# A Macaron layer with a selective scan: giving its two FFNs row buffers of their own, and carrying rows and scan output through DRAM

## The chip, the cores and the metric

The kernel runs on one core of a Trainium2 chip. The metric is device microseconds of one execution; the median of several runs is given. One further execution was recorded by the hardware profiler; the profile below is of that one.

## What is computed

The input x has 2 sequences of 2048 positions and 1024 features, all in float32. Three residual steps follow each other:

```
x = x + 0.5 * ffn(layernorm(x))
x = x + mamba(layernorm(x))
x = x + 0.5 * ffn(layernorm(x))
```

Both FFNs have the same weights. For each position, `ffn` forms 64 vectors of 16 numbers (one 1024x1024 product with A), takes the 4 vectors with the largest norm, sums those 4 into one vector v, spreads it over the chosen ones, and returns `x W^T + bias + (spread v) B`: three 1024x1024 products in all. `mamba` projects to a step delta (rank 128, then softplus) and to B and C of 16 states, and runs

```
h[t] = exp(delta[t] * A) * h[t-1] + delta[t] * B[t] * x[t]
y[t] = sum over the 16 states of h[t] * C[t];   result: y + x * D_param
```

over the positions, for 1024 features x 16 states, starting at zero in each sequence.

## The kernel before, in words

The 4096 positions are cut into 16 chunks of 256, each of two row blocks of 128 positions. A row block lies in an SBUF tile x of 128 positions x 1024 features. For every chunk the program adds tasks in this order: `ffn("f", c, i)` for both row blocks (the first FFN), `prepare(c)`, `scans(c)`, and `ffn("g", c, i)` for both (the second FFN).

- `ffn` (from L486). An f block is loaded in two layouts by `load_rows` (L337): as rows (x) and transposed (xnt). A g block takes the x tile that the scan has added to, and turns it with 8 PE transposes (`turn`, L464). Statistics are made by DVE and ACT (L424 to L446). PE computes the products with A (wa), W (ww) and B (wb), all at L515, 16 of 128x512 each; each product leaves two records in the profile. In between ACT squares (L537), DVE selects (L551 to L574) and POOL spreads (L583). DVE adds the result into the x tile (`close`, L601), and a g block is stored (L613).
- `prepare` (from L619) normalizes the chunk's x, turns it into u, projects it, makes delta, and stores delta, u*delta, u, B and C in DRAM tiles (du_d, u_d, bc_d).
- `scans` (from L760) goes through 1024 features in four steps of two 128-feature blocks (q). In each it fetches du_d back, replicated fourfold over the partitions, into four rep tiles, and runs 16 tasks (4 groups of states hi x 4 groups of features j). A task is: ACT's exponential (`decay`, L808), DVE's product (`entry`, L816), DVE's recurrence (`scan`, L823, two instructions), ACT's copy of the last state (L833), POOL's product with C (`leave`, L836). After every four tasks PE sums states into y (L856). At the end of a step DVE adds u * D_param to y (`skip`, L869), PE turns the result (`back`, L877), and DVE adds it into the two x tiles of the chunk (`summed`, L886).

So an x tile is held from the load of an f block until the store of the same g block. There are six such tiles, and the f blocks of a chunk can be at most three chunks ahead of the g blocks.

The order on each engine is fixed before the kernel is built. Each task names an engine, a planned cost in us, what it reads and writes, a rank, and the places of pools it takes and gives back. `Plan.order` (L124) plays the program through with these costs: whenever an engine is free it takes the ready task of lowest rank whose places are free. DVE and POOL tasks marked `port` are not started while the other engine has such a task running. A transfer's places and results count as there when its planned landing time has passed. The tasks are then emitted in the order found, and on the chip each engine works through its own list strictly in that order, waiting where something isn't there yet. All transfers are issued by SP's queue.

Pools that matter: x 6; xnt 2; rep 5; h 10 (a task's state tile, given back by PE's sum at L856); ysb 2; the PSUM pools ff 3 and pt 2; the DRAM pools du_d, u_d and bc_d, 2 each. The rank of an f block comes from a list (`f_seq`, L329) in which the f blocks of chunk c + 3 stand beside the g blocks of chunk c.

Of the kernel before, what the change touches and what calls it, by code (L numbers as in the profile page):

```python
# [28 lines left out]
FP = mybir.dt.float32  # L29
# [6 lines left out]
P = 128  # L36
TC = 256
# [187 lines left out]
def macaron_kernel(  # L225
# [39 lines left out]

    places("x", 6, [P, D])
    places("row", 1, [P, D])
# [59 lines left out]

    xs, xts, ready = {}, {}, {}
    f_seq = [("f", c, i) for c in range(min(3, NCH)) for i in range(NT)]  # L329
# [7 lines left out]
    def load_rows(c, i):  # L337
        xs[c, i] = x_p = Place("x")
# [12 lines left out]

# [67 lines left out]
    def spread_of(x_p, st, factor, rank, after=()):  # L419
# [27 lines left out]

        add("DVE", 1.9, stats, row(x_p) + list(after), [(st, 0)], rank=-40.0 + rank, take=[st])
        add("ACT", 1.8, root, [(st, 0)], [(st, 1)], rank=-10.0 + rank)

    def normalize(x_p, xn_p, rank, after=()):

        st = Place("stats")
        spread_of(x_p, st, 1.0, rank, after)

        def scale():
            r, s = st.tile[:, 15:16], st.tile[:, 16:17]
            nc.scalar.activation(s, st.tile[:, 13:14], AF.Identity, scale=r)
            nc.scalar.activation(xn_p.tile, x_p.tile, AF.Identity, bias=s, scale=r)

        add("ACT", 1.45, scale, row(x_p) + [(st, 1)], [(xn_p, 0), (xn_p, 1)], rank=-10.0 + rank,
            take=[xn_p], give=[st])

    def turn(src, keys, dst, out_keys, rank, take=(), give_src=None):  # L464

        for g in range(2):
            pt = Place("pt")

            def pe(g=g, pt=pt):
                for k in range(HC):  # L470
                    c0 = (g * HC + k) * P
                    nc.tensor.transpose(  # L472
                        pt.tile[:, k * P : (k + 1) * P], src.tile[:, c0 : c0 + P], ident
                    )
# [4 lines left out]
            add("PE", 0.65, pe, keys(g) + ([(take[0], "-")] if take and g else []), [(pt, 0)],  # L479
                rank=-50.0 + rank, take=[pt] + (list(take) if g == 0 else []),  # L480
                give=[src] if give_src else [])
            add("ACT", 0.58, act, [(pt, 0)], out_keys(g), rank=-60.0 + rank, give=[pt])

    def ffn(kind, c, i):  # L486
        n = place_in[kind, c, i]
        rank = 0.01 * n
        if kind == "f":
            load_rows(c, i)  # L490
        x_p = xs[c, i]
        g_p, gt, ch, mk, st = (Place(k) for k in ("g", "gt", "choice", "marked", "stats"))
# [10 lines left out]
        for h in range(2):  # L503
            def bias(h=h):
                cols = slice(h * HD, (h + 1) * HD)
                nc.gpsimd.tensor_add(x_p.tile[:, cols], x_p.tile[:, cols], half_bias[:, cols])  # L506

            add("POOL", 1.3, bias, row(x_p, h) + ["half_bias"], row(x_p, h), rank=rank, port=True)
        turn_of = Turn()

        def products(ps, h, lhs, w, wn, start, stop, order, take, give, after=()):
            for k4 in range(KC // 4):
                def pe(k4=k4):
# [8 lines left out]

                add("PE", 3.6, pe,
                    [(lhs, k4)] + [(wn, k, h) for k in range(4 * k4, 4 * k4 + 4)]
# [21 lines left out]
        def choose():  # L546
# [12 lines left out]

        add("DVE", 2.2, choose, [(g_p, 0), (g_p, 1)], [(ch, 0)], rank=-50.0 + rank,  # L560
            take=[ch, mk], give=[mk])
        for h in range(2):
            def routed(h=h):
# [5 lines left out]

            add("DVE", 0.68, routed, [(pv[h], 0), (ch, 0)], [(g_p, h)], rank=-50.0 + rank,  # L570
                give=[pv[h]])
# [6 lines left out]

        add("DVE", 1.25, total, [(g_p, 0), (g_p, 1)], [(ch, 1)], rank=-50.0 + rank)
        for h in range(2):  # L580
            def spread(h=h):
# [6 lines left out]

            add("POOL", 1.3, spread, [(ch, 0), (ch, 1)], [(g_p, h)], rank=-30.0 + rank, port=True,
                give=[ch])  # L590
# [5 lines left out]
        for h in range(2):  # L596
            products(po, h, gt, wb, "wb", False, True, lambda: turn_of.number - 1000.0, [], [gt])

            def close(h=h):
# [5 lines left out]

            add("DVE", 0.68, close, [(po[h], 0), (st, 1)] + row(x_p, h), row(x_p, h),
                rank=-50.0 + rank, give=[po[h], st])
        if kind == "g":
            b, t = chunks[c]
# [9 lines left out]
    def prepare(c):  # L619
# [48 lines left out]
        def keep(p, pt, m):  # L668
            return lambda: nc.scalar.copy(p.tile[:m, :], pt.tile[:m, :TC])

        add("PE", 3.8, project, ["wx"] + u_all, [(pd, 0)], rank=-45.0 + rank, take=[pd])
        add("ACT", 0.38, keep(dr, pd, P), [(pd, 0)], [(dr, 0)], rank=-55.0 + rank, take=[dr],
            give=[pd])
        add("PE", 1.3, project_bc, ["wx"] + u_all, [(pb, 0)], rank=-45.0 + rank, take=[pb])
        add("ACT", 0.38, keep(bc, pb, P), [(pb, 0)], [(bc, 0)], rank=-55.0 + rank, take=[bc],
# [11 lines left out]
        for g in range(2):  # L687
            dg, e = Place("delta"), Place("row")
            for k2 in range(HC // 2):
# [10 lines left out]
                def parts(g=g, k2=k2, pt=pt, e=e, dg=dg):  # L700
# [5 lines left out]

                add("PE", 0.8, pz, [(dr, 0), "wdt"] + ([(e, "-")] if k2 else []), [(pt, 0)],
                    rank=-45.0 + rank, take=[pt] if k2 else [pt, e, dg], give=[dr])
                add("ACT", 1.85, parts, [(pt, 0), "bdt"], [(e, k2), (dg, k2)], rank=-55.0 + rank,
                    give=[pt])  # L710
# [29 lines left out]
            ukeys = [(u, g, i) for i in range(NT)]  # L740
            add("ACT", 1.1, exp, ek, ek, rank=-20.0 + rank)
# [3 lines left out]
            add("ACT", 3.7, log, ek, ek, rank=-20.0 + rank)  # L745
            add("DVE", 1.25, delta, ek + dk, dk, rank=-20.0 + rank, port=True, give=[e])
# [13 lines left out]
    def scans(c):  # L760

        du_d, bc_d, u_d = ready.pop(c)
        bs, cs = [Place("b") for _ in range(HI)], [Place("c") for _ in range(HI)]
        for hi in range(HI):
# [9 lines left out]
        for q in range(0, KC, 2):  # L774
            reps = [Place("rep") for _ in range(NJ)]
            for j in range(NJ):
                def fetch(q=q, j=j, r=reps[j]):
# [11 lines left out]
                    give=[du_d], land=4.0)  # L789
            y, ysb, pt = Place("y"), Place("ysb"), Place("pt")  # L790

# [8 lines left out]
            for hi in range(HI):  # L800
                hs = []
                for j in range(NJ):
# [32 lines left out]
                    def leave(h=h, hi=hi):  # L835
# [6 lines left out]
                    end = q == KC - 2  # L842
                    add("ACT", 1.0, decay, [(r, 0), "a_neg"], [(da, 0)], rank=-80.0 + rank, take=[da],
                        give=[r])
# [3 lines left out]
                    add("DVE", 1.36, scan, [(da, 0), (h, 0), key], [(h, 0)], rank=rank, give=[da])  # L848
                    add("ACT", 0.2, keep, [(h, 0)], [key, (h, 1)], rank=-90.0 + rank)
# [13 lines left out]

                add("PE", 1.0, total, [(h, 0) for h in hs], [(y, 0)], rank=-70.0 + rank,
                    take=[y] if hi == 0 else [], give=hs)
# [100 lines left out]
```

## Time and profile before

| | us |
|---|---|
| median of 3 runs | 3503.4 |
| lowest, highest | 3498.0, 3507.41 |
| the profiled execution, its own time | 3495.17 |
| its span in the profile | 3493.4 |
| mean granted TensorE clock | 0.986 |

The page of the profile lists, for each engine, its busy time in the span (PE is TensorE's matmuls, PEld its weight loads, DVE VectorE, ACT ScalarE, POOL GpSimd, SP SyncE), then 40 slices of the span with the busy share of each engine in tenths (9 is 90% or more), and the granted clock of TensorE in tenths. "Chain" is the work that ended last, followed back from the end. A group's line has its line in the kernel, engine and operation, the tiles it writes and reads, its shape and count; then busy time and the mean duration of one in ns; then the idle time of the engine ahead of it and what ended most of that. A queue's name with a q (SPq) means its sequencer.

Transfers take a 24% share of the 16 DMA engines over the span and move 285.70 MB. Median times from issue to landing: rep<-du_d 3.3 us, x<-in_x 4.5, ysb<-u_d 2.8, out<-x 2.6.

### The profile page before, as it was taken

To read this page: it belongs to the slowest core of one execution; us is meant where nothing else is said; L and a number is where in the kernel's file an instruction comes from. 1 tells how busy PE (TensorE), PEld (TensorE's weight loads), DVE (VectorE), ACT (ScalarE), POOL (GpSimd) and SP (SyncE) were. 2 spreads that over 40 slices of the span, in tenths; PEclk is the share of its full clock that TensorE was granted. 3 is DMA by queue.
4 is the path that set the end of the run, shared out by engine and by line. 5 is a ranking of instruction groups with operands and counts; after the bars stand their busy time and mean duration, and the time that the engine had idled before them with its cause. 6 is when DMAs were issued, how large, how long until landed. Compare 5 with 4: busy or idle time off the path is not lost.

```text
span 3493.4 us, 36224 instructions
## 1 busy us (share of the span) xinstructions
PE 3309.1 (95%) x10280; PEld 1456.1 (42%) x10280; DVE 3136.3 (90%) x4753; ACT 1882.0 (54%) x4818; POOL 1882.0 (54%) x1299
## 2 busy tenths in 40 slices
PE   7999798999998999999999999999999999999989
PEld 3444333444443444443443444444444444444434
DVE  5399999999999999998899999898989989899991
ACT  1365655556465555655564655565565555555541
POOL 1154566555465665645555566464555655465571
PEclk9999899999999999999999999999999999999999
DMA  5222222222223213222131221312222232222210
GB/s 201 90 71 81 96 82 67 94 85 67 80 77 99 73 62 112 70 85 82 58 103 61 97 82 58 124 58 97 67 97 70 69 110 69 95 70 74 72 58 12
DMA packets 182058, 285.70 MB, mean 82 GB/s; under 512 B 17120, under 2 KB 100704, under 8 KB 181856
## 3 DMA queue, kind: packets, MB, share of 16 engines
q1 hardware_dynamic: 181856, 283.38, 24.2%
q8 instruction: 81, 1.33, 0.2%
q14 instruction: 121, 0.99, 0.1%
HBM read 215.69 MB, written 67.63 MB: 81 GB/s over the span
## 4 chain that ended last, share of the span: by engine, by line
PE 44%; DVE 33%; issue 11%; ACT 9%; DMA 2%; SPq 0%; POOL 0%; DVEq 0%; POOLq 0%; ACTq 0%
PE ff L515 37%; DVE h L823 14%; DVE h L816 7%; PE y L856 3%; DVE stats L424 2%; ACT da L808 2%; ACT stats L445 1%; DVE norms L551 1%; DVE g L564 1%; PE pt L472 1%; ACT stats L446 1%; PE pt L695 1%; DMA rep<-du_d 1%; DVE x L601 1%; DVE x L886 1%
## 5 line engine op out<-in xcount | busy, mean ns | idle before, releaser
L836 POOL TENSOR_TENSOR h<-h,c 128x512 f32<-128x512 f32 x1024 | 1544.1, 1518 | 1057.2 <-ACT state L833 1002.2
L808 ACT ACTIVATE da<-rep,a_neg 128x256 f32<-128x256 f32 x2048 | 974.6, 477 | 956.0 <-DVE h L823 916.3
L823 DVE TENSOR_TENSOR_SCAN h<-da,state,h 128x256 f32<-128x256 f32 x2048 | 1384.4, 727 | 23.1 <-ACT da L808 19.3
L816 DVE TENSOR_TENSOR h<-rep,b 128x512 f32<-128x512 f32 x1024 | 968.6, 973 | 61.0 <-PE y L856 59.0
L515 PE MATMUL ff<-ww,xnt 128*128 128x512 f32 x2048 | 908.4, 600 | 28.6 <-DVE g L564 28.1
L515 PE MATMUL ff<-wa,xnt 128*128 128x512 f32 x2048 | 918.4, 597 | 0.4 <-ACT xnt L477 0.2
L515 PE MATMUL ff<-wb,gt 128*128 128x512 f32 x2048 | 899.0, 597 | 16.1 <-ACT gt L477 16.0
L515 PEld LDWEIGHTS ff<-ww,xnt 128*128 128x128 f32 x2048 | 390.7, 192 | 535.9 <-issue 476.7
L515 PEld LDWEIGHTS ff<-wb,gt 128*128 128x128 f32 x2048 | 386.8, 191 | 489.0 <-issue 460.1
L515 PEld LDWEIGHTS ff<-wa,xnt 128*128 128x128 f32 x2048 | 378.0, 190 | 480.6 <-issue 475.3
L583 POOL TENSOR_TENSOR g<-choice 128x512 f32<-128x512 f32 x128 | 162.9, 1292 | 323.9 <-DVE choice L574 323.9
L856 PE MATMUL y<-h,summer 128*32 128x512 f32 x2048 | 305.0, 609 | 30.1 <-POOL h L836 26.9
L506 POOL TENSOR_TENSOR x<-x,half_bias 128x512 f32<-128x512 f32 x128 | 173.6, 1368 | 186.9 <-DVE stats L424 164.0
L833 ACT COPY state<-h 128x2 f32<-128x2 f32 x1024 | 186.3, 182 | 110.1 <-DVE h L823 109.7
L537 ACT ACTIVATE g<-ff 128x512 f32<-128x512 f32 x128 | 133.7, 1046 | 115.7 <-PE ff L515 115.1
L601 DVE SCALAR_TENSOR_TENSOR x<-ff,stats,x 128x512 f32<-128x512 f32 x128 | 93.6, 732 | 81.8 <-PE ff L515 81.0
L424 DVE BATCH_NORM_STATS2 stats<-x 128x6 f32<-128x512 f32 x192 | 122.3, 677 | 40.5 <-DMA x<-in_x 40.4
L856 PEld LDWEIGHTS y<-h,summer 128*32 128x32 f32 x2048 | 51.6, 109 | 220.3 <-POOL h L836 111.0
L477 ACT COPY gt<-pt 128x512 f32<-128x512 f32 x128 | 69.8, 584 | 101.6 <-PE pt L472 101.6
L444 ACT ACTIVATE stats<-stats 128x1 f32<-128x1 f32 x288 | 58.2, 202 | 121.7 <-DVE stats L436 115.6
L445 ACT ACTIVATE stats<-stats,less 128x1 f32<-128x1 f32 x288 | 111.3, 386 | 9.7
L551 DVE TENSOR_REDUCE norms<-g 128x64 f32<-128x1024 f32 x64 | 76.8, 1199 | 27.0 <-ACT g L537 21.8
(73 smaller groups left out, 1753.2 us busy)
## 6 DMA issues: line engine op xcount, KB each, us to landing
rep<-du_d SPq DMA_DIRECT2D x512, 256.0 KB, 3.3
xnt<-in_x_t SPq DMA_DIRECT2D x32, 512.0 KB, 3.6
x<-in_x SPq DMA_DIRECT2D x32, 512.0 KB, 4.5
u_d<-u SPq DMA_DIRECT2D x32, 512.0 KB, 4.7
ysb<-u_d SPq DMA_DIRECT2D x64, 256.0 KB, 2.8
du_d<-delta SPq DMA_DIRECT2D x32, 512.0 KB, 3.2
du_d<-u SPq DMA_DIRECT2D x32, 512.0 KB, 3.0
out<-x SPq DMA_DIRECT2D x32, 512.0 KB, 2.6
```

The costliest lines, as they stand in the source:

```text
L424: nc.vector.bn_stats(st.tile[:, 6 * s : 6 * s + 6], x_p.tile[:, s * HD : (s + 1) * HD])
L445: nc.scalar.activation(t, q, AF.Identity, bias=less, scale=hv)
L506: nc.gpsimd.tensor_add(x_p.tile[:, cols], x_p.tile[:, cols], half_bias[:, cols])
L515: nc.tensor.matmul(ps[h].tile, lhsT=lhs.tile[:, k, :], rhs=w[:, k, h * HD : (h + 1) * HD], start=start and k == 0, stop=stop and k == KC - 1,)
L537: nc.scalar.activation(g_p.tile.rearrange("p (a r) -> p r a", r=RANK)[:, h * r2 : (h + 1) * r2, :], vecs(pv, h), AF.Square,)
L583: nc.gpsimd.tensor_mul(g_p.tile[:, h * HD : (h + 1) * HD].rearrange("p (r a) -> p r a", a=na), ch.tile[:, :NA].unsqueeze(1).to_broadcast([ ...
L808: nc.scalar.activation(da.tile[:, k, :], r.tile[:, k, 0, :], AF.Exp, scale=a_neg[:, q + k, j, hi : hi + 1],)
L816: nc.vector.tensor_mul(h.tile, r.tile[:, :, 1, :], bs[hi].tile.unsqueeze(1).to_broadcast([P, 2, TC]),)
L823: nc.vector.tensor_tensor_scan(h.tile[:, k, :], da.tile[:, k, :], h.tile[:, k, :], state[:, q + k, j, hi : hi + 1], ALU.mult, ALU.add,)
L833: nc.scalar.copy(state[:, q : q + 2, j, hi : hi + 1], h.tile[:, :, TC - 1 : TC])
L836: nc.gpsimd.tensor_mul(h.tile, h.tile, cs[hi].tile.unsqueeze(1).to_broadcast([P, 2, TC]))
L856: nc.tensor.matmul(y.tile[j * DB : (j + 1) * DB, :], lhsT=summer, rhs=hs[j].tile.rearrange("p k t -> p (k t)"), start=(hi == 0), stop=(hi ...
```

## The change

The six x tiles become three xf (first FFN), two xg (second FFN) and one yt (a row block's y, features on partitions). After `close`, an f block is stored in a DRAM tile x1_d, and its xf tile is given back when this store has landed and `prepare` has normalized it. The scan no longer turns y nor adds it: each step stores its y in a DRAM tile y_d. A new function `load_sum` fetches a g block's x and y, turns y in two groups of four transposes, and adds it to x. The DRAM pools du_d, u_d and bc_d have four tiles instead of two. Some 30 planned costs are altered; those move the order alone.

```diff
-    places("x", 6, [P, D])
+    places("xf", 3, [P, D])
+    places("xg", 2, [P, D])
+    places("yt", 1, [P, KC, P])
...
-    plan.pool("du_d", [dram.tile([D, 2, TC], FP, name=f"du_d{j}") for j in range(2)])
-    plan.pool("u_d", [dram.tile([D, TC], FP, name=f"u_d{j}") for j in range(2)])
-    plan.pool("bc_d", [dram.tile([2 * N, TC], FP, name=f"bc_d{j}") for j in range(2)])
+    plan.pool("du_d", [dram.tile([D, 2, TC], FP, name=f"du_d{j}") for j in range(4)])
+    plan.pool("u_d", [dram.tile([D, TC], FP, name=f"u_d{j}") for j in range(4)])
+    plan.pool("bc_d", [dram.tile([2 * N, TC], FP, name=f"bc_d{j}") for j in range(4)])
+
+    plan.pool("x1_d", [dram.tile([P, D], FP, name=f"x1_d{j}") for j in range(2 * NT * 4)])
+    plan.pool("y_d", [dram.tile([D, TC], FP, name=f"y_d{j}") for j in range(4)])
...
+    def load_sum(c, i, rank):
+
+        xs[c, i] = x_p = Place("xg")
+        yt = Place("yt")
+        x1_d, y_d = x1_ds.pop((c, i)), y_ds[c]
+
+        def fetch_x():
+            nc.sync.dma_start(out=x_p.tile, in_=x1_d.tile)
+
+        def fetch_y():
+            nc.sync.dma_start(
+                out=yt.tile,
+                in_=y_d.tile[:, i * P : (i + 1) * P].rearrange("(k p) t -> p k t", p=P),
+            )
+
+        add("SP", 0.4, fetch_x, [(x1_d, 0)] + [(y_d, q) for q in range(0, KC, 2)], row(x_p),
+            rank=-30.0 + rank, take=[x_p], give=[x1_d], land=3.0)
+        add("SP", 0.6, fetch_y, [(y_d, q) for q in range(0, KC, 2)], [(yt, 0)], rank=-30.0 + rank,
+            take=[yt], give=[y_d], land=4.0)
+        for g in range(2):
+            pt = Place("pt")
+
+            def back(g=g, pt=pt):
+                for k in range(HC):
+                    nc.tensor.transpose(
+                        pt.tile[:, k * P : (k + 1) * P], yt.tile[:, g * HC + k, :], ident
+                    )
+
+            def summed(g=g, pt=pt):
+                cols = x_p.tile[:, g * HD : (g + 1) * HD]
+                nc.vector.tensor_add(cols, pt.tile, cols)
+
+            add("PE", 0.56, back, [(yt, 0)] + row(x_p, g), [(pt, 0)], rank=-50.0 + rank, take=[pt], give=[yt])
+            add("DVE", 0.72, summed, [(pt, 0)] + row(x_p, g), row(x_p, g), rank=-45.0 + rank,
+                give=[pt])
...
-        add("ACT", 1.8, root, [(st, 0)], [(st, 1)], rank=-10.0 + rank)
+        add("ACT", 2.65, root, [(st, 0)], [(st, 1)], rank=-10.0 + rank)
...
-            take=[xn_p], give=[st])
+            take=[xn_p], give=[st, x_p])
...
+        else:
+            load_sum(c, i, rank)
...
-                add("PE", 3.6, pe,
+                add("PE", 3.44, pe,
...
-        if kind == "g":
+        if kind == "f":
+            x1_ds[c, i] = x1_d = Place("x1_d")
+
+            def keep():
+                nc.sync.dma_start(out=x1_d.tile, in_=x_p.tile)
+
+            add("SP", 0.4, keep, row(x_p), [(x1_d, 0)], rank=-50.0, take=[x1_d], give=[x_p],
+                land=3.0)
+        else:
...
-                    add("DVE", 0.68, entry, [(r, 0), (bs[hi], 0)], [(h, 0)], rank=rank - 0.0012,
+                    add("DVE", 0.66, entry, [(r, 0), (bs[hi], 0)], [(h, 0)], rank=rank - 0.0012,
...
-                    add("POOL", 1.3, leave, [(h, 1), (cs[hi], 0)], [(h, 0)], rank=-20.0 + rank,
+                    add("POOL", 1.26, leave, [(h, 1), (cs[hi], 0)], [(h, 0)], rank=-20.0 + rank,
...
-            def back(ysb=ysb, pt=pt):
-                for i in range(NT):
-                    for k in range(2):
-                        nc.tensor.transpose(
-                            pt.tile[:, (2 * i + k) * P : (2 * i + k + 1) * P],
-                            ysb.tile[:, k, i * P : (i + 1) * P],
-                            ident,
-                        )
-
-            def summed(q=q, pt=pt):
-                for i in range(NT):
-                    cols = xs[c, i].tile[:, q * P : (q + 2) * P]
-                    nc.vector.tensor_add(cols, pt.tile[:, 2 * i * P : 2 * (i + 1) * P], cols)
-
-            add("DVE", 0.8, skip, [(y, 0), (ysb, 0), "d_col"], [(ysb, 0)], rank=-45.0, give=[y])
-            add("PE", 0.65, back, [(ysb, 0)], [(pt, 0)], rank=-75.0 + rank, take=[pt], give=[ysb])
-            add("DVE", 0.84, summed, [(pt, 0)],
-                [(xs[c, i], k) for i in range(NT) for k in (q, q + 1)], rank=-45.0, give=[pt])
+            def put_y(q=q, ysb=ysb):
+                nc.sync.dma_start(
+                    out=y_d.tile[q * P : (q + 2) * P, :].rearrange("(k p) t -> p k t", p=P),
+                    in_=ysb.tile,
+                )
+
+            add("DVE", 0.86, skip, [(y, 0), (ysb, 0), "d_col"], [(ysb, 0)], rank=-45.0, give=[y])
+            add("SP", 0.4, put_y, [(ysb, 0)], [(y_d, q)], rank=-50.0, take=[] if q else [y_d],
+                give=[ysb], land=3.0)
```

More of the change, by code (lines that the diff above doesn't have):

```diff
@@ L326, in macaron_kernel @@
     plan.pool("marked", marked)
-    xs, xts, ready = {}, {}, {}
+    xs, xts, ready, x1_ds, y_ds = {}, {}, {}, {}, {}
     f_seq = [("f", c, i) for c in range(min(3, NCH)) for i in range(NT)]
@@ L337, in load_rows @@
     def load_rows(c, i):
-        xs[c, i] = x_p = Place("x")
+        xs[c, i] = x_p = Place("xf")
         xts[c, i] = xt = Place("xnt")
@@ L446, in root @@
                 nc.scalar.activation(r, t, AF.Identity, scale=r)
-        add("DVE", 1.9, stats, row(x_p) + list(after), [(st, 0)], rank=-40.0 + rank, take=[st])
-        add("ACT", 1.8, root, [(st, 0)], [(st, 1)], rank=-10.0 + rank)
+        add("DVE", 1.94, stats, row(x_p) + list(after), [(st, 0)], rank=-40.0 + rank, take=[st])
+        add("ACT", 2.65, root, [(st, 0)], [(st, 1)], rank=-10.0 + rank)
     def normalize(x_p, xn_p, rank, after=()):
@@ L459, in scale @@
             nc.scalar.activation(xn_p.tile, x_p.tile, AF.Identity, bias=s, scale=r)
-        add("ACT", 1.45, scale, row(x_p) + [(st, 1)], [(xn_p, 0), (xn_p, 1)], rank=-10.0 + rank,
-            take=[xn_p], give=[st])
+        add("ACT", 1.55, scale, row(x_p) + [(st, 1)], [(xn_p, 0), (xn_p, 1)], rank=-10.0 + rank,
+            take=[xn_p], give=[st, x_p])
     def turn(src, keys, dst, out_keys, rank, take=(), give_src=None):
@@ L477, in act @@
                 nc.scalar.copy(dst(g), pt.tile.rearrange("p (k t) -> p k t", k=HC))
-            add("PE", 0.65, pe, keys(g) + ([(take[0], "-")] if take and g else []), [(pt, 0)],
+            add("PE", 0.56, pe, keys(g) + ([(take[0], "-")] if take and g else []), [(pt, 0)],
                 rank=-50.0 + rank, take=[pt] + (list(take) if g == 0 else []),
                 give=[src] if give_src else [])
-            add("ACT", 0.58, act, [(pt, 0)], out_keys(g), rank=-60.0 + rank, give=[pt])
+            add("ACT", 0.585, act, [(pt, 0)], out_keys(g), rank=-60.0 + rank, give=[pt])
     def ffn(kind, c, i):
@@ L506, in bias @@
                 nc.gpsimd.tensor_add(x_p.tile[:, cols], x_p.tile[:, cols], half_bias[:, cols])
-            add("POOL", 1.3, bias, row(x_p, h) + ["half_bias"], row(x_p, h), rank=rank, port=True)
+            add("POOL", 1.26, bias, row(x_p, h) + ["half_bias"], row(x_p, h), rank=rank, port=True)
         turn_of = Turn()
@@ L558, in choose @@
             nc.vector.tensor_scalar(routes, routes, CHOSEN, 1.0 / TOPK, ALU.is_equal, ALU.mult)
-        add("DVE", 2.2, choose, [(g_p, 0), (g_p, 1)], [(ch, 0)], rank=-50.0 + rank,
+        add("DVE", 2.24, choose, [(g_p, 0), (g_p, 1)], [(ch, 0)], rank=-50.0 + rank,
             take=[ch, mk], give=[mk])
@@ L568, in routed @@
                 )
-            add("DVE", 0.68, routed, [(pv[h], 0), (ch, 0)], [(g_p, h)], rank=-50.0 + rank,
+            add("DVE", 0.65, routed, [(pv[h], 0), (ch, 0)], [(g_p, h)], rank=-50.0 + rank,
                 give=[pv[h]])
@@ L577, in total @@
             )
-        add("DVE", 1.25, total, [(g_p, 0), (g_p, 1)], [(ch, 1)], rank=-50.0 + rank)
+        add("DVE", 1.22, total, [(g_p, 0), (g_p, 1)], [(ch, 1)], rank=-50.0 + rank)
         for h in range(2):
@@ L587, in spread @@
                 )
-            add("POOL", 1.3, spread, [(ch, 0), (ch, 1)], [(g_p, h)], rank=-30.0 + rank, port=True,
+            add("POOL", 1.26, spread, [(ch, 0), (ch, 1)], [(g_p, h)], rank=-30.0 + rank, port=True,
                 give=[ch])
@@ L604, in close @@
                 )
-            add("DVE", 0.68, close, [(po[h], 0), (st, 1)] + row(x_p, h), row(x_p, h),
+            add("DVE", 0.73, close, [(po[h], 0), (st, 1)] + row(x_p, h), row(x_p, h),
                 rank=-50.0 + rank, give=[po[h], st])
-        if kind == "g":
+        if kind == "f":
[5 more added lines that the diff above has]
+        else:
             b, t = chunks[c]
@@ L669, in keep @@
             return lambda: nc.scalar.copy(p.tile[:m, :], pt.tile[:m, :TC])
-        add("PE", 3.8, project, ["wx"] + u_all, [(pd, 0)], rank=-45.0 + rank, take=[pd])
+        add("PE", 3.6, project, ["wx"] + u_all, [(pd, 0)], rank=-45.0 + rank, take=[pd])
         add("ACT", 0.38, keep(dr, pd, P), [(pd, 0)], [(dr, 0)], rank=-55.0 + rank, take=[dr],
             give=[pd])
-        add("PE", 1.3, project_bc, ["wx"] + u_all, [(pb, 0)], rank=-45.0 + rank, take=[pb])
+        add("PE", 1.05, project_bc, ["wx"] + u_all, [(pb, 0)], rank=-45.0 + rank, take=[pb])
         add("ACT", 0.38, keep(bc, pb, P), [(pb, 0)], [(bc, 0)], rank=-55.0 + rank, take=[bc],
@@ L705, in parts @@
                         nc.scalar.activation(dg.tile[:, k, :], z, AF.Relu, bias=bias)
-                add("PE", 0.8, pz, [(dr, 0), "wdt"] + ([(e, "-")] if k2 else []), [(pt, 0)],
+                add("PE", 0.93, pz, [(dr, 0), "wdt"] + ([(e, "-")] if k2 else []), [(pt, 0)],
                     rank=-45.0 + rank, take=[pt] if k2 else [pt, e, dg], give=[dr])
-                add("ACT", 1.85, parts, [(pt, 0), "bdt"], [(e, k2), (dg, k2)], rank=-55.0 + rank,
+                add("ACT", 1.92, parts, [(pt, 0), "bdt"], [(e, k2), (dg, k2)], rank=-55.0 + rank,
                     give=[pt])
@@ L740, in prepare @@
             ukeys = [(u, g, i) for i in range(NT)]
-            add("ACT", 1.1, exp, ek, ek, rank=-20.0 + rank)
+            add("ACT", 1.06, exp, ek, ek, rank=-20.0 + rank)
             add("DVE", 1.25, plus, ek + dk, dk, rank=-20.0 + rank, port=True)
@@ L744, in prepare @@
             add("DVE", 1.25, rest, ek + dk, dk, rank=-20.0 + rank, port=True)
-            add("ACT", 3.7, log, ek, ek, rank=-20.0 + rank)
+            add("ACT", 3.6, log, ek, ek, rank=-20.0 + rank)
             add("DVE", 1.25, delta, ek + dk, dk, rank=-20.0 + rank, port=True, give=[e])
@@ L762, in scans @@
         du_d, bc_d, u_d = ready.pop(c)
+        y_ds[c] = y_d = Place("y_d")
         bs, cs = [Place("b") for _ in range(HI)], [Place("c") for _ in range(HI)]
@@ L789, in scans @@
                     give=[du_d], land=4.0)
-            y, ysb, pt = Place("y"), Place("ysb"), Place("pt")
+            y, ysb = Place("y"), Place("ysb")
             def fetch_u(q=q, ysb=ysb):
@@ L842, in scans @@
                     end = q == KC - 2
-                    add("ACT", 1.0, decay, [(r, 0), "a_neg"], [(da, 0)], rank=-80.0 + rank, take=[da],
+                    add("ACT", 0.955, decay, [(r, 0), "a_neg"], [(da, 0)], rank=-80.0 + rank, take=[da],
                         give=[r])
-                    add("DVE", 0.68, entry, [(r, 0), (bs[hi], 0)], [(h, 0)], rank=rank - 0.0012,
+                    add("DVE", 0.66, entry, [(r, 0), (bs[hi], 0)], [(h, 0)], rank=rank - 0.0012,
                         take=[h], port=True,
                         give=[r] + ([bs[hi]] if end else []))
-                    add("DVE", 1.36, scan, [(da, 0), (h, 0), key], [(h, 0)], rank=rank, give=[da])
-                    add("ACT", 0.2, keep, [(h, 0)], [key, (h, 1)], rank=-90.0 + rank)
-                    add("POOL", 1.3, leave, [(h, 1), (cs[hi], 0)], [(h, 0)], rank=-20.0 + rank,
+                    add("DVE", 1.352, scan, [(da, 0), (h, 0), key], [(h, 0)], rank=rank, give=[da])
+                    add("ACT", 0.185, keep, [(h, 0)], [key, (h, 1)], rank=-90.0 + rank)
+                    add("POOL", 1.26, leave, [(h, 1), (cs[hi], 0)], [(h, 0)], rank=-20.0 + rank,
                         port=True, give=[cs[hi]] if end else [])
@@ L862, in total @@
                         )
-                add("PE", 1.0, total, [(h, 0) for h in hs], [(y, 0)], rank=-70.0 + rank,
+                add("PE", 0.99, total, [(h, 0) for h in hs], [(y, 0)], rank=-70.0 + rank,
                     take=[y] if hi == 0 else [], give=hs)
```

## The prediction, made before the changed kernel was run

> **What bounds the kernel now.** I read the page's busy shares and its chain first, then the slices, then busy time by stretch, then the groups.
>
> ```profile
> PE 3309.1 (95%) x10280; PEld 1456.1 (42%) x10280; DVE 3136.3 (90%) x4753; ACT 1882.0 (54%) x4818; POOL 1882.0 (54%) x1299
> ...
> PE   7999798999998999999999999999999999999989
> ...
> DVE  5399999999999999998899999898989989899991
> ...
> PEclk9999899999999999999999999999999999999999
> ...
> PE 44%; DVE 33%; issue 11%; ACT 9%; DMA 2%; SPq 0%; POOL 0%; DVEq 0%; POOLq 0%; ACTq 0%
> ```
>
> PE is busy for 3309 of 3493.4 us and the chain runs over PE and DVE in turn, so neither alone is the bound and transfers (2%) are not. The time is therefore three stages: until chunk 0 of the scan ends, the other 15 chunks, and what is left after the last. Their borders are the chunk's last skip operation (L869) in the timeline: 389, 1799 (chunk 7), 3227 (chunk 14) and 3408 us (chunk 15). Busy time between them (columns: stretch, length, then each engine's busy us and records, granted clock, DMA share, GB/s):
>
> ```profile
> 175.00:389.00 214.00, 186.77 (x599) 80.88 (x598) 207.05 (x294) 133.12 (x329) 110.92 (x74) 0.96 0.25 83
> 389.00:1799.00 1410.00, 1331.57 (x4169) 584.50 (x4170) 1342.21 (x2004) 783.88 (x2032) 811.80 (x553) 0.98 0.25 81
> 1799.00:3227.00 1428.00, 1396.74 (x4438) 618.39 (x4437) 1327.95 (x2040) 813.61 (x2084) 812.50 (x557) 1.00 0.24 80
> 3227.00:3408.00 181.00, 164.47 (x483) 66.08 (x481) 166.47 (x256) 93.14 (x239) 113.40 (x74) 0.98 0.20 67
> 3408.00:3493.40 85.40, 79.99 (x204) 36.21 (x203) 16.33 (x35) 12.32 (x28) 9.02 (x8) 1.00 0.03 13
> ```
>
> Two regimes. In the first seven chunks DVE is the busier engine (1342 against 1332 us of 1410; 201 us a chunk) and PE has holes. In the next seven PE is at 98% (1397 of 1428; 204 us a chunk). After the last scan PE does FFNs alone for 85 us. The groups that fill these stretches:
>
> ```profile
> L823 DVE TENSOR_TENSOR_SCAN h<-da,state,h 128x256 f32<-128x256 f32 x2048 | 1384.4, 727 | 23.1 <-ACT da L808 19.3
> L816 DVE TENSOR_TENSOR h<-rep,b 128x512 f32<-128x512 f32 x1024 | 968.6, 973 | 61.0 <-PE y L856 59.0
> L515 PE MATMUL ff<-ww,xnt 128*128 128x512 f32 x2048 | 908.4, 600 | 28.6 <-DVE g L564 28.1
> L856 PE MATMUL y<-h,summer 128*32 128x512 f32 x2048 | 305.0, 609 | 30.1 <-POOL h L836 26.9
> L601 DVE SCALAR_TENSOR_TENSOR x<-ff,stats,x 128x512 f32<-128x512 f32 x128 | 93.6, 732 | 81.8 <-PE ff L515 81.0
> ```
>
> The entry (L816) averages 973 ns, but in the timeline an undisturbed one takes 0.66 us; the rest is waiting for the port that it shares with POOL's products (L836).
>
> **The change, part by part.** Its arithmetic hardly changes. *Turning y:* four 128x128 transposes for each two d-blocks of a chunk (L877, 42.5 us in all) become eight for each row block: 256 records before and after, so 0. *The sum:* 128 adds of 128x256 (46.9 us) become 64 of 128x512. I price one as L601, the same shape with one PSUM operand: 0.73 us, so 47 us, or 0. The lower bound is two halves of L886 without their second start, about 0.68 (-3 us). The upper is the entry's 0.97 us, if it had to wait for POOL: +15 us. The Trainium skill (SBUF — State Buffer, Who interferes with whom) says that a DVE instruction with at most one SBUF input does not contend with GpSimd; L886 agrees (387 to 425 ns in all 128), so I take 0.
>
> *Transfers:* 32 stores and 32 loads of x (512 KB), 64 stores of y (256 KB) and 32 loads of it: 160 issues at about 0.4 us (the trace's x load and output store: medians 0.42 and 0.36) are 64 us of SP in 3493, and 67 MB on 285.7, so a DMA share of some 30% instead of 24%. Hidden unless a wait in SP's queue reaches the scan's fetches; that is a rival below. Uncovered, one g row would pay a store's landing (2.6), a fetch (4.5 as x<-in_x, the same size; at most twice ysb<-u_d's 2.8, which has half the bytes) and the turning and adding, 2.6: 10 to 12 us. The turning waits for both fetches at PE, and behind it in PE's order stand the other row's FFN products and the scan's y products, which give DVE its h places back. It is covered because xg has two places: the other row's FFN is 48 products of 128x512 at 0.887 x 0.975, about 42 us of PE.
>
> *The order* is what really changes, because x places no longer tie an FFN to the one three chunks later, and the DRAM pools go from 2 to 4. I counted each kernel's built order by stage, multiplying every row by its group's busy time over its count: DVE scan 0.676, entry 0.946, PE 128x512 product 0.887 (two records), y product 0.298, the others likewise. The sums overrate slightly, since neighbouring records overlap, so they are calibrated on before.
>
> Before, PE: chunk 0 333, then 195, 195, 185, 192, 193, 186, 210, 187, six of 211, 158, and 82 after the last scan. The 82 was 80.0 us busy: factor 0.975. DVE: chunk 0 293 (78 of it before the first scan), then 200, 203, 189, 199, 202, 193, 205, 186, six of 203, 183. The first five of these sum to 992 and took 1000 us (389 to 1389): 1.008; the last took 181 for 183: 0.99.
>
> After, PE: chunk 0 363, then 217, 195, 174, 201, 189, 196, 173, 200, 189, 191, 187, 190, 181, 195, 188, and **151** after the last scan. DVE: 295 (82 before the first scan), then 225, 202, 188, 210, 202, 201, 195, 209, 202, 198, 188, 198, 178, 194, 172.
>
> So FFN work moves from the middle to the two ends. In the middle PE has 0.975 x 2792 = 2722 us to do and DVE 2962 order units: DVE binds in all but the last chunk, and what PE could gain there is lost.
>
> Summing the stages:
> - Chunk 0 ends at 389 before. DVE has 3.7 us more ahead of the first scan and 2 less behind it: 390. PE's 0.975 x 363 = 354 plus some 25 us of missing weights at the start (slice 1: 62.8 busy of 87.3) is 379, beneath it.
> - Fifteen chunks: DVE's 2962 at a factor between 0.99 and 1.008; I take 1.00. In the last chunk PE has 183 against DVE's 172, so +11: 2973. Before took 3019, so 46 us are won.
> - After the last scan: 0.975 x 151 = 147, plus 3 for the last store and 3 for starting, as 80.0 became 85.4: 153, which is 68 us more.
>
> 390 + 2973 + 153 = 3516 us of span. The profile of before took 3495.2 for a span of 3493.4, so 3518; and it lies 8 below the median of the runs (3503.4). The forecast is **3525 us** for the median, 0.6% slower.
>
> *The new costs in the planner* remove no work. Root's 1.8 to 2.65 is nearer the measured 2.65 (3 x 0.88) and the rest are within a few per cent of rows; their effect is in the order counted above, with one thing left open: collisions at the port.
>
> The Trainium skill (TensorE: Matmul & The Clock Gate, What's actually happening) speaks against giving PE holes: after an idle window of about 3.4 us it passes half the clock. The row: the clock is 0.98 over 389 to 1799, or 28 us in seven chunks, 4 us a chunk. PE has 2962 - 2722 = 240 us of slack in fifteen chunks, 16 a chunk, so by the row nothing is added. By the rule, were all 16 us such windows, five of them, each costs 1.7 us of PE work: 8.5, also within it. I add 0; only in the last chunk and the tail would it show.
>
> **The rivals.**
>
> *Fewer collisions (faster).* Place: L816 waiting for POOL's L836. In the first seven chunks entries average about 1.02 us, in the later ones 0.93, in the last 0.85. If closer planning costs give the last figure for every chunk, DVE loses 64 x (0.946 - 0.85) = 6 us in each of 14, 86 us, of which PE's floors give back some 10: 3525 - 76 = 3449. With still fewer, PE's sums end it near 3420. It decides above 2 us a chunk (32 us). For: costs nearer the rows. Against: which operation stands before an entry tells its wait in before (second entry in a row after a scan 1.14 us, after entry and scan 0.76), and after's order has no better mix: weighted by it, 0.989 against 0.974. Also, DVE was most often hit exactly where it was densest.
>
> *Gain and tail cancel.* DVE's factor is 0.992, as in the last chunk, instead of 1: 24 us less, 3501, no change that can be told.
>
> *SP's queue (much slower).* SP is in order. Behind an x fetch that waits for a store to land, or a y fetch that waits for the turning before it, stand the rep fetches. A rep place freed in the last quarter of a step is wanted five tasks later, 15 us at 3.1 a task, and its own fetch takes 4.4: 10 us of slack. SP already waits 300 us for stores (29 times) and DVE waits only 1.9 for rep. If one in two of the 64 new fetches overruns by 2.5 us, that is 80 us: 3605.
>
> *The lead isn't used.* Then the tail would stay at 82 and DVE's chunks at 203; the counted order excludes it.
>
> **How the numbers follow.** My own sum 0.38, the SP queue 0.14, cancelling 0.20, fewer collisions 0.28. A measurement of this kernel tells about 0.3% from no change, so faster is below 3493, same up to 3514. Faster 0.28, same 0.19, slower 0.53. The range of my own sum is 3514 to 3555 (factor up to 1.008, sum +15). The range that should hold it 8 times in 10 reaches from 3430, inside the collision case, to 3600.
>
> **What would show it.** Right: the last skip operation of chunk 15 ends near 3363, some 45 earlier than now, with 150 us of PE alone behind it; DVE at 95% or more and PE near 92% in the chunks; the clock lower there. Wrong, first step: chunks at 190 us and entries below 0.9 us mean the collision rival. DVE idle before the entries, released by rep's DMA, for tens of us means SP's queue. If PE has holes in the tail, the two xg places don't cover those 12 us.

## The result and the profile after

The changed kernel takes 3520.0 us (median of 5 runs, 3519.24 to 3529.56) against 3501.57 (5 runs): 1.0059 times the time before, 95% interval 1.0041 to 1.0078. Forecast were 3525. Before itself took 3501 us beside experiments 4, 5 and 8, 3539 beside 2, 3 and the first halves of 1 and 7, and 3544 beside 6 and the second halves of 1 and 7, and the unaltered changed kernel ran only where before took 3501, so a ratio from one group is set beside one from another only with that caution.

The page's lines that answer to those shown of before:

```profile
PE 3314.0 (94%) x10280; PEld 1462.4 (42%) x10280; DVE 3147.2 (89%) x4689; ACT 1873.0 (53%) x4818; POOL 1908.4 (54%) x1299
...
PE   7998999999899999999899989999998999999999
...
DVE  5289999999999999999999999999999999999921
...
PEclk9999999999899999999999999999999999999999
...
PE 40%; DVE 39%; issue 13%; ACT 5%; DMA 3%; SPq 0%; DVEq 0%; POOL 0%; ACTq 0%
```

Nothing was added to PE or DVE to speak of (+5 and +11 us). DVE's row is now nines to the end, with two thin slices behind it instead of one, and in the chain DVE has come level with PE. Busy time by stretch, cut at the ends of chunks 0, 7, 14 and 15 of the scan as before:

```profile
188.00:406.80 218.80, 204.92 (x643) 90.54 (x642) 212.48 (x310) 131.47 (x337) 122.63 (x82) 0.97 0.31 104
406.80:1824.10 1417.30, 1325.31 (x4199) 585.89 (x4198) 1370.34 (x2022) 849.21 (x2176) 823.86 (x548) 0.97 0.32 106
1824.10:3182.60 1358.50, 1299.69 (x4083) 566.93 (x4082) 1298.11 (x1933) 740.44 (x1928) 817.76 (x552) 0.98 0.30 99
3182.60:3367.90 185.30, 180.84 (x573) 78.28 (x571) 165.35 (x252) 84.69 (x229) 109.88 (x74) 0.99 0.22 71
3367.90:3517.80 149.90, 144.47 (x377) 66.50 (x376) 25.49 (x49) 17.54 (x36) 11.20 (x10) 0.99 0.09 30
```

| stage, us | before | forecast | after |
|---|---|---|---|
| until chunk 0 ends | 389 | 390 | 406.8 |
| chunks 1 to 7 | 1410 | 1423 | 1417.3 |
| chunks 8 to 14 | 1428 | 1367 | 1358.5 |
| chunk 15 | 181 | 183 | 185.3 |
| behind the last scan | 85 | 153 | 149.9 |
| span | 3493.4 | 3516 | 3517.8 |

(The forecast's chunks are its stage sums, added up.) The whole gain, 70 us, lies in chunks 8 to 14. PE was busy for 98% of them before; it now is for 96% of a shorter stretch. The gain is given back behind the last scan (65 us), ahead of the end of chunk 0 (18 us), and in chunks 1 to 7 and 15 (7 and 4 us). In PE's account, idle time went from 184 to 204 us (from 31 to 59 in chunks 8 to 14), and the granted clock from 0.986 to 0.979.

The FFN products alone show what moved. First before, then the changed kernel: until chunk 0 ends, the other fifteen chunks, behind the last scan (busy time and records of PE and PEld, clock, DMA share, GB/s).

```profile
0.00:388.80 388.80, 261.33 (x592) 112.45 (x592) 0.97 0.32 111
388.80:3408.00 3019.20, 2376.82 (x5376) 1009.89 (x5376) 0.99 0.24 80
3408.00:3493.40 85.40, 76.33 (x176) 33.19 (x176) 1.00 0.03 13
...
0.00:406.80 406.80, 302.30 (x676) 130.22 (x677) 0.97 0.35 124
406.80:3367.90 2961.10, 2289.57 (x5150) 972.72 (x5148) 0.98 0.30 101
3367.90:3517.80 149.90, 138.86 (x320) 60.17 (x320) 0.99 0.09 30
```

The middle lost 87 us of PE's FFN work and became only 58 us shorter; the two ends got 41 and 63 us of it and became 18 and 65 us longer.

DVE's and POOL's groups in the middle, and the waits of SP's queue for transfers, which were the rivals' ground:

```profile
L888 POOL TENSOR_TENSOR h<-h,c 128x512 f32<-128x512 f32 x1024 | 1561.6, 1535 | 1079.7 <-ACT state L885 1005.2
...
L868 DVE TENSOR_TENSOR h<-rep,b 128x512 f32<-128x512 f32 x1024 | 984.3, 989 | 14.1 <-PE y L908 14.1
```

```profile
SPq L845 <- DMA y_d<-ysb: 109.3, 53, 4.6
...
SPq L363 <- DMA out<-xg: 41.0, 21, 4.7
```

The entry (L868) was 973 ns and is 989: collisions with POOL did not become fewer. SP does stand waiting for landings (the columns are us in all, times, longest): at 53 of the 64 fetches into ysb, behind a store of y, and at 21 of the 32 x fetches, behind a store of a finished row block. But no idle time of DVE is put down to rep's fetches at all, where before had 1.9 us.

### The profile page after: what moved, and what is told of

Same layout as the page of the kernel before. It is cut to its first block, busy times and chain, and to the rows that moved or that the text cites. A ratio compares the mean times of both kernels' runs of the same rounds, so it can differ in the third digit from the quotient of the medians.

```text
span 3517.8 us, 36497 instructions
## 1 busy us (share of the span) xinstructions
PE 3314.0 (94%) x10280; PEld 1462.4 (42%) x10280; DVE 3147.2 (89%) x4689; ACT 1873.0 (53%) x4818; POOL 1908.4 (54%) x1299
## 4 chain that ended last, share of the span: by engine, by line
PE 40%; DVE 39%; issue 13%; ACT 5%; DMA 3%; SPq 0%; DVEq 0%; POOL 0%; ACTq 0%
PE ff L558 35%; DVE h L875 18%; DVE h L868 9%; PE y L908 2%; DVE g L607 2%; ACT da L860 1%; DVE norms L594 1%; DVE stats L465 1%; PE pt L513 1%; DMA xf<-in_x 1%; DVE ysb L921 1%; DVE delta L771 1%; DVE choice L601 1%; DVE choice L617 1%; DMA yt<-y_d 1%
## 5 line engine op out<-in xcount | busy, mean ns | idle before, releaser
L888 POOL TENSOR_TENSOR h<-h,c 128x512 f32<-128x512 f32 x1024 | 1561.6, 1535 | 1079.7 <-ACT state L885 1005.2
L868 DVE TENSOR_TENSOR h<-rep,b 128x512 f32<-128x512 f32 x1024 | 984.3, 989 | 14.1 <-PE y L908 14.1
L558 PE MATMUL ff<-wb,gt 128*128 128x512 f32 x2048 | 918.6, 607 | 32.0 <-ACT gt L518 32.0
L908 PE MATMUL y<-h,summer 128*32 128x512 f32 x2048 | 296.4, 617 | 14.9 <-POOL h L888 9.3
L644 DVE SCALAR_TENSOR_TENSOR xg<-ff,stats,xg 128x512 f32<-128x512 f32 x64 | 47.3, 739 | 106.9 <-PE ff L558 106.4
L549 POOL TENSOR_TENSOR xg<-xg,half_bias 128x512 f32<-128x512 f32 x64 | 88.9, 1399 | 81.0 <-PE pt L513 80.8
L465 DVE BATCH_NORM_STATS2 stats<-xf 128x6 f32<-128x512 f32 x128 | 81.3, 676 | 47.4 <-DMA xf<-in_x 47.3
L513 PE MATMUL pt<-ident,g 128*128 128x128 f32 x512 | 78.4, 292 | 44.1 <-ACT xnt L518 12.8
L549 POOL TENSOR_TENSOR xf<-xf,half_bias 128x512 f32<-128x512 f32 x64 | 89.0, 1411 | 56.2 <-DVE stats L465 56.0
```

The lines of the kernel that those rows point to most:

```text
L465: nc.vector.bn_stats(st.tile[:, 6 * s : 6 * s + 6], x_p.tile[:, s * HD : (s + 1) * HD])
L513: nc.tensor.transpose(pt.tile[:, k * P : (k + 1) * P], src.tile[:, c0 : c0 + P], ident)
L558: nc.tensor.matmul(ps[h].tile, lhsT=lhs.tile[:, k, :], rhs=w[:, k, h * HD : (h + 1) * HD], start=start and k == 0, stop=stop and k == KC - 1,)
L868: nc.vector.tensor_mul(h.tile, r.tile[:, :, 1, :], bs[hi].tile.unsqueeze(1).to_broadcast([P, 2, TC]),)
L888: nc.gpsimd.tensor_mul(h.tile, h.tile, cs[hi].tile.unsqueeze(1).to_broadcast([P, 2, TC]))
L908: nc.tensor.matmul(y.tile[j * DB : (j + 1) * DB, :], lhsT=summer, rhs=hs[j].tile.rearrange("p k t -> p (k t)"), start=(hi == 0), stop=(hi ...
```

## Experiments

**1. The planning costs alone.** The kernel before with the changed numbers and nothing else (25 edits of one kind):

```diff
-        add("ACT", 1.8, root, [(st, 0)], [(st, 1)], rank=-10.0 + rank)
+        add("ACT", 2.65, root, [(st, 0)], [(st, 1)], rank=-10.0 + rank)
...
-                add("PE", 3.6, pe,
+                add("PE", 3.44, pe,
```

> The kernel before with the new planning costs and nothing else of the change. The built order has 82 us of PE work after the last scan, as before, and stage sums that differ from before's by less than 10 us in total (mid-stage bound 3007 against 2992, first chunk 382 against 389). If the loss comes from the order that the separate row buffers allow (my theory): within 0.3% of before, 3490 to 3515, the tail after the last scan 85 us. If the new costs are what makes it slower (rival): about 3520, half a per cent above before.

Measured: 3512.9 us, 0.993 of before (0.9912 to 0.9947; before 3539.4 beside it). So the new costs alone are not what makes it slower: the rival is out, but my theory's "within 0.3%" is missed too. It was run again:

> The kernel before with the new planning costs, once more, because it was 0.7% below before where before itself took 3539 us instead of 3500. If the gain is the order's own, about 0.993 of before here too (3475); if it is that before was slow on the earlier chip, about 3513, 1.003.

Measured: 3511.4 us, 0.9904 (0.9885 to 0.9922; before 3544.3). The ratio is that of a gain, 0.7 to 1% in the two runs; the microseconds are those of no gain, because before took 3544 again. Whether these costs would beat a before of 3501 us was not tried. The tail is 85.2 us, as counted. One thing is settled: the first entry starts at 188 us, as in the changed kernel, and not at 171. Chunk 0 nevertheless ends at 388 and 390 us in these two runs, as in before: its own stretch is shorter by as much.

**2. The places and transfers alone.** The changed kernel with the old costs (the reverse of the edits above).

> The changed kernel with the planning costs of before wherever an operation exists in both. Its built order has 196 us of PE work after the last scan (151 in the changed kernel, 82 in before), and the smallest sums in the middle. My theory (FFN work that leaves the middle is lost, since VectorE binds there): first chunk 390 to 407, middle 2955, tail 197, together 3540 to 3560, slower than the changed kernel. The rival (new costs are the loss, the buffers a gain): faster than before, 3480 or less.

Measured: 3561.4 us, 1.0064 (1.0042 to 1.0086; before 3539.4). First entry at 171 us; chunk 0 ends at 385, 5 us under the range that I gave; middle 2983 (28 over its sum), tail 193 (4 under). So the change is slower with the old costs too, and the loss is in what the buffers allow. Which part of them was not separated: the four DRAM tiles instead of two for du_d, u_d and bc_d were never run alone.

**3. Half of POOL's product, in the changed kernel.** The second half of the positions isn't multiplied by C.

```diff
-                            h.tile, h.tile, cs[hi].tile.unsqueeze(1).to_broadcast([P, 2, TC])
+                            h.tile[:, :, : TC // 2], h.tile[:, :, : TC // 2],
+                            cs[hi].tile[:, : TC // 2].unsqueeze(1).to_broadcast([P, 2, TC // 2]),
```

> The changed kernel with POOL's product with C over only the first half of each task's positions; the other half is left unmultiplied. Planned costs and so the order are untouched. It halves the time that POOL holds the port. If VectorE, with its waits for the port, binds the fifteen middle chunks (2961 us in the changed kernel), entries fall from 0.99 to about 0.80 us and the middle shrinks by 64 x 0.19 = 12 us a chunk, 150 to 180 in all, until PE's 2792 is met: middle 2790 to 2840, total 3360 to 3400. If PE or the transfers bind it, the middle stays above 2930.

Measured: 3406.2 us, 0.9628 (0.961 to 0.9646; before 3539.4). The two groups of this kernel:

```profile
L888 POOL TENSOR_TENSOR h<-h,c 128x256 f32<-128x256 f32 x1024 | 975.9, 954 | 1418.6 <-DVE h L875 1273.3
...
L868 DVE TENSOR_TENSOR h<-rep,b 128x512 f32<-128x512 f32 x1024 | 828.2, 837 | 27.9 <-PE y L909 27.8
```

The entry lost 152 ns though nothing of it was altered, 156 us over 1024 of them, and the middle went from 2961 to 2861 us, 20 above the range that I gave. Fourteen of the fifteen chunks became shorter, by 2 to 12 us. So DVE's waits at the port are on the path in the whole middle, and about two thirds of what they lose there is time lost.

**4. The same edit in the kernel before.**

> The kernel before with POOL's product with C over only the first half of each task's positions; the rest is left unmultiplied. The order is that of before. In the changed kernel the same edit took 4.3% (1.0059 to 0.9628 of before). My theory says that before is bound by VectorE for seven chunks only and by PE at 98% for seven others: it gains less, 2 to 3.3% (about 3385 to 3430 where before takes 3502), with chunks 8 to 14 still above 200 us and chunks 1 to 7 near 190. The rival that both kernels are bound alike: 4.3%, chunks 8 to 14 near 193.

Measured: 3390.1 us, 0.9682 (0.9666 to 0.9698; before 3500.9). Chunks 1 to 7, 8 to 14 and 15 of this kernel, and below them chunks 8 to 14 of experiment 3:

```profile
372.20:1721.00 1348.80, 1307.37 (x4165) 581.87 (x4165) 1241.43 (x2002) 781.72 (x2031) 557.50 (x552) 0.99 0.26 85
1721.00:3127.00 1406.00, 1387.52 (x4442) 619.63 (x4443) 1262.71 (x2040) 810.15 (x2085) 551.38 (x557) 1.00 0.25 82
3127.00:3306.40 179.40, 164.08 (x484) 66.06 (x482) 165.49 (x256) 92.99 (x239) 72.32 (x74) 0.97 0.19 64
...
1758.30:3074.00 1315.70, 1284.42 (x4083) 563.55 (x4082) 1232.59 (x1933) 738.98 (x1929) 553.38 (x550) 0.99 0.31 102
```

DVE was relieved by 101 us in before's first seven chunks (1342 us busy to 1241) and by 65 in the next seven; the first gave 61 us of time, the next only 22, and those stay at 201 us a chunk with PE busy for 98.7%. In the changed kernel the same relief of 65 us in chunks 8 to 14 gave 43. That is the two regimes of the prediction: PE bounds chunks 8 to 14 of before, and in the changed kernel it bounds them no longer. The totals do not show it: in microseconds both kernels gained much the same, 111 us here and 114 in experiment 3, and the 4.3% from which the expectation sets out rests on before's 3539 us there.

**5. A shorter lead of the first FFN.** Two chunks in the list of ranks, not three.

```diff
-    f_seq = [("f", c, i) for c in range(min(3, NCH)) for i in range(NT)]
+    f_seq = [("f", c, i) for c in range(min(2, NCH)) for i in range(NT)]
...
-            if c + 3 < NCH:
-                f_seq.append(("f", c + 3, i))
+            if c + 2 < NCH:
+                f_seq.append(("f", c + 2, i))
```

> The changed kernel with the list of ranks putting the first FFN two chunks ahead of the second instead of three. The built order has 92 us of PE work after the last scan (151 in the changed kernel) and 2923 in the middle (2864). If PE work in the middle is free there because VectorE binds (my theory), the tail falls to 96 us and the middle hardly grows (by the stage sums 3014 instead of 2972): total 3500, 0.3 to 0.6% below the changed kernel. The rival, that work put back into the middle costs its full time: middle 3020 or more, total as the changed kernel.

Measured: 3622.7 us, 1.0353 (1.0336 to 1.037; before 3500.9). The tail did fall, to 103 us. But chunk 15 took 274 us, and two stretches, at its start and behind, tell why:

```profile
3240.00:3345.00 105.00, 102.28 (x306) 49.96 (x299) 23.09 (x41) 25.34 (x54) 7.88 (x7) 1.00 0.22 74
3345.00:3515.80 170.80, 134.32 (x341) 44.62 (x339) 156.96 (x233) 84.00 (x219) 114.25 (x70) 0.92 0.21 69
```

For 105 us PE did FFNs and DVE next to nothing: the chunk's delta and u were not there yet, since its first FFN came too late. Stage sums do not see that; they assume that a scan's input is there. And the fourteen chunks ahead of it, with 94 more FFN records on PE than the unaltered kernel of experiment 8 has there (4896 and 4802, some 40 us at 0.429 us a record), were 66 us longer (2837 against 2771). So the step "PE work in the middle is free there" is wrong as I put it: the rival's outcome, full time and more, came true. Whether the work itself costs this, or the places that the new order gives it, is not separated.

**6. Another order of the same work.** The planner's time from engine to engine at 0.15 instead of 0.25 us.

> The changed kernel with 0.15 us instead of 0.25. The order changes alone: 92 us of PE work after the last scan instead of 151, 2909 instead of 2864 in the middle. If the loss of the changed kernel is where its order puts the FFNs, the tail of 150 us falls to 96: stage sums first chunk 398 to 415, middle 2994, tail 96, total 3487 to 3510, below the changed kernel by 0.3 to 0.9%. If the loss is in the buffers or transfers themselves, total 3515 or more.

Measured: 3567.1 us, 1.0054 (1.0034 to 1.0073; before 3544.3). Tail 102, middle 3042, chunk 0 ends at 420. The tail gave 48 us, and the middle and chunk 0 took 81 and 13. Less the 43 us by which before was longer beside it, 51 of these 94 remain, so the tail's gain was used up all the same. That is the outcome that I had put down to the buffers or transfers themselves, and not the gain that I expected. Experiment 7 leaves little for the transfers; which of the buffers it would be is not shown.

> The kernel before with the planner's time from one engine to another put at 0.15 us instead of 0.25 (in the trace, POOL starts 0.17 us after ACT's copy, and ACT 0.18 us after VectorE's scan). Nothing but the order changes. Stage sums of the built order: first chunk 385, middle 2983 (before 2992), after the last scan 86. The sums underrated before by 26 us, so 3454 + 26 = 3480, 0.6% below before. If orders of equal sums differ by how the queues mesh, which sums cannot see, it may lie 1% to either side.

Measured in the kernel before: 3551.5 us, 1.0018 (1.0009 to 1.0027): no gain, with a middle of 3073, 90 us above its sum. Against experiment 1 (0.9904 beside the same before), sums of nearly equal size gave times a full per cent apart, as allowed for. The changed kernel's agreement to 2 us is closer than the method is.

**7. Are the transfers hidden?** Each new transfer issued twice, to the same places:

> The changed kernel with each of the new transfers (row store and fetch, y store and fetch) issued twice, to the same places: another 160 issues and 67 MB. My theory (they are hidden): within 0.3% of the changed kernel, 3515 to 3530, and no idle time of VectorE's entries put down to rep's DMA. The rival that SP's queue and traffic cost something already: at least another 20 us, 3540 or more.

Measured: 3597.6 us, 1.0168 (1.015 to 1.0186; before 3539.4). That looked like a price for traffic, until SP's waits were read:

```profile
SPq L937 <- DMA y_d<-ysb: 145.1, 64, 5.5
SPq L371 <- DMA yt<-y_d: 143.5, 32, 5.8
SPq L364 <- DMA xg<-x_d: 111.4, 32, 4.8
...
SPq L661 <- DMA x_d<-xf: 83.3, 32, 4.7
```

A repeat to the same tile waits until the first has landed, 160 times, 483 us in all, with everything behind it in SP's queue. So the bytes were doubled once more without that wait, into tiles that nothing reads:

```diff
+            nc.sync.dma_start(out=next_spare("x"), in_=x1_d.tile)
...
+                nc.sync.dma_start(out=next_spare("x"), in_=x_p.tile)
```

(and likewise for y).

> The changed kernel with every new transfer issued a second time into DRAM tiles that nothing reads: 160 more issues and as many bytes as the new transfers, but no repeat waits for the landing of its first, as it did in the run with doubled transfers (1.0168 of before, SP held for 483 us by those landings). If it was that waiting in SP's queue that cost 38 us, this one lies within 0.4% of the changed kernel, 1.004 to 1.010 of before. If it is the traffic or the issuing, 1.014 to 1.019, and then the new transfers of the change itself cost about as much.

Measured: 3544.1 us, 0.9996 (0.9987 to 1.0006; before 3544.3). With 420 MB moved instead of 353 it is 54 us below the run with landings waited for. The cost there was waiting in SP's queue, 54 us for 483 us of it, and not traffic or issuing. Against the changed kernel's 3520 us it is 24 us more, but beside a before that was 43 us longer: if whatever lengthened before does not shorten this kernel, the price of the doubled traffic is at most 24 us. The ratio is below that of the changed kernel, against all that I expected. Unless more traffic helps, before and the changed kernel are not slowed alike where before takes 3544 us.

**8. Both kernels once more.**

> The kernel before, unaltered, profiled on the chip of these runs, because it took 3539 us on the chip of the last ones and 3502 on the first. If the chips differ in how fast an engine works, the mean of the scan operation (727 ns) or of a 128x512 product differs; if they differ in latencies alone, those are equal and the middle stage (3019 us on the first chip) is longer by the difference.

Before, one profiled execution: 3489.0 us, first chunk 388, middle 3014, tail 85. On this same chip before later took 3544, so it is not the chip. Nor is it the granted clock: its mean was 0.986 both where before took 3501 us and where it took 3539. In the variants run there the scan operation averages 727 to 728 ns, as ever, and PE's 128x512 records follow each other in 0.429 us in all profiles. What differs is open; before itself has no profile of such a run.

> The changed kernel, unaltered, on the same chip as its variants. My theory: 0.6% above before, tail 150 us, middle about 2960. If the doubled transfers of the earlier run cost nothing, it lies about 1.7% above before on the chip where they did; if they cost what that run suggests (38 us), 0.6% above.

The changed kernel: 3520.6 us, 1.0059 (1.0041 to 1.0077; before 3500.9), middle 2958, tail 149.9: the result again. It does not settle whether the doubled transfers cost anything, since before took 3501 us here and 3539 there.

## Why the prediction was right

The account of the middle and the tail was right. That the total came out to 2 us is luck: one term was 17 us too small, and two others were 12 and 3 us too large.

- **Regimes.** Right, and shown by the stages of experiments 3 and 4. DVE at 95% or more in the changed kernel's chunks: 1370 of 1417 (97%) and 1298 of 1358 (96%).
- **Middle.** Forecast 2973, measured 2961. DVE's order units needed a factor of 0.996 in chunks 1 to 7 and 0.994 in 8 to 14, where I had taken 1.00; in the last chunk PE took 181 us of 185, as forecast.
- **Tail.** Forecast 153, measured 149.9: the 147 of PE's work and the 3 of the last store, without the 3 set aside for starting. The two xg places covered the fetches: no hole in the last two slices, and in the whole kernel DVE and PE waited 2.8 and 2.0 us for x and y fetches.
- **Chunk 0.** Forecast 390, measured 406.8: this term was mis-sized by 17 us. The first entry starts at 188.3 us and not at about 175. I had counted DVE's work ahead of it and missed what stands ahead of chunk 0's projection in PE's order: 20 FFN products instead of 4. The changed kernel's PE, and below it before's, where the projection reads u:

```profile
130.22 3.60 PE L558 MATMUL ff<-wa,xnt 128*128 128x512 f32 x8
133.65 13.90 PE L558 MATMUL ff<-ww,xnt 128*128 128x512 f32 x32
147.39 3.62 PE L697 MATMUL pt<-u,wx 128*128 128x256 f32 x16
```

```profile
127.06 3.60 PE L515 MATMUL ff<-wa,xnt 128*128 128x512 f32 x8
130.50 3.62 PE L646 MATMUL pt<-u,wx 128*128 128x256 f32 x16
```

  Experiments 1 and 2 put the late start on the planning costs: the projection starts at 147.4 and 131.0 us there, the first entry at 188 and 171. But chunk 0's end moved only with both: 388 us with the costs alone, 385 with the places alone, 407 together. The line of the prediction that only collisions were left open about the costs missed this.
- **Gain and tail cancel.** This rival was closer than the total shows. Its factor was 0.992; measured over chunks 1 to 14 is 0.995, more than half of the way to it. By the same sum, without the 17 us of chunk 0 the changed kernel would have taken some 3503 us against 3501, no change that can be told. That it is slower beyond the noise was forecast from the tail and came from the tail and chunk 0 together.
- **Errors of arithmetic.** After's PE sums for the middle add to 2866 (2864 before rounding), not 2792; 2792 is already 0.975 of it, and I multiplied twice. PE's need is 2792 (2806 busy in the profile), its slack 170 us, not 240, and "PE near 92%" should have been 94% (measured 95%). The time did not use it; the weighing of the clock rule did, with 16 us of slack a chunk where there were 11. The collision rival set the entry's busy time over its count, 0.946, against the last chunk's mean duration, 0.85; busy time over count in the last chunk is 0.817, so that rival was worth 116 us and not 86. And the range with a factor of 1.008 and the sum at +15 ends at 3564, not 3555. None of the three changes the forecast.
- **"What PE could gain there is lost."** Too strong. Experiments 5 and 6 put 40 to 46 us of PE work back into the middle (94 and 108 records), and the middle grew by 66 (over 14 chunks) and 81 us, the latter where before itself was 43 us longer. In fixed orders the two engines wait for each other: in chunks 8 to 14 both are at 96%, and neither has free time that another order simply gets. What the change does is to trade 58 us of middle for 65 of tail and 18 ahead of it. The three other orders tried of the separate buffers (experiments 2, 5, 6) took 3561 to 3623 us, all above 3520.
- **The sum operation.** All 64 took 654 to 692 ns, and half of them ran mostly while a product of POOL was running:

```profile
L386 DVE TENSOR_TENSOR xg<-pt,xg x64: 654/675/692, 417.4 to 3437.9; 128x512 f32<-128x512 f32 x64
```

  So it did not wait for the port: the rule of the Trainium skill that I had gone by (SBUF — State Buffer, Who interferes with whom) held, at the lower of my two bounds.
- **The clock.** I had added nothing, and the middle came out at the sum. The clock did go down, 0.986 to 0.979, some 25 us of full-speed time over the span ((0.986 - 0.979) x 3518). That this lies within PE's slack is argued, not shown by a run.
- **Rivals.** Fewer collisions: no, 989 ns. SP's queue: its mechanism is real (experiment 7: 54 us for 483 us of waits), but in the change SP's waits for landings are some 180 us (56 in before), many of them short, and all engines together waited 3.0 us for rep's fetches (12.5 in before).

## What to carry to other kernels

Where two engines share a statically ordered kernel, count each engine's work between fixed points of the built order, calibrate on the kernel that you have, and take the larger for each stage: work that leaves the middle for the end is paid there. Here such sums missed the middle by 12 us in the forecast and by about 1 to 3% in the five other orders of experiments 1, 2, 5 and 6. Look beside the sum for the few instructions ahead of the stage that starts everything, and for inputs that come too late, because it sees neither. A buffer that lets one engine run ahead shortens a stage only until the next engine bounds it: here 87 us of PE work left the middle and 58 us of time.

## What was not expected of the hardware

- POOL's and DVE's port cost more than any edit of the order gained: halving POOL's product took 111 and 114 us off the two kernels, with DVE's own instructions unaltered (entry 973 to 813 ns in before, 989 to 837 in the changed kernel).
- Waiting in SP's queue cost a ninth of its length: 483 us of waits for landings cost 54 us of time, and 67 MB more without those waits cost at most 24.
- The granted clock follows PE's idle time: over the fourteen profiles it falls from 0.990 with 125 us idle (experiment 4) to 0.972 with 265 us idle (experiment 5). This is a correlation; no experiment altered the idle time alone.
